# A Mamba scan on one core: three accumulating transfers and a gate moved in the issue order

## The chip, the cores and the metric

The kernel runs on one core of one Trainium2 chip. The metric is the device time of one execution in microseconds (us), lower is better. A profiled execution gives, for each instruction, its engine, start and duration. The engines are PE (matrix multiply, with its weight loads as a row of their own, PEld), DVE (vector), ACT (scalar, activation functions), POOL (general) and SP (issues transfers). Each engine takes its instructions strictly in its own order; an instruction that must wait for a semaphore holds up everything behind it on that engine.

## The reference, cut to what matters

The network has four layers: a double Mamba block, a convolution with attention over taps, a linear attention with a mixture of experts, and a softmax attention with a mixture of experts. The change lies in the first layer alone. What a Mamba block computes, with 512 inner channels, 16 states and sequences of 1024 tokens in 2 images:

```python
delta = softplus(dt @ dt_w + dt_b)
dA = exp(delta[..., None] * A)                      # per token, channel, state
dBu = delta[..., None] * Bm[:, :, None, :] * xs[..., None]
h = dA_t * h + dBu_t                                # a scan over the tokens
y_t = einsum('bdn,bn->bd', h, C_t)                  # sum over the 16 states
y = (y + xs * Dp) * silu(res)                       # res is the gate
out = y @ out_w + out_b
```

The block is applied twice (m1, m2), each time followed by a layer norm and a residual sum.

## The kernel before, in words

**Tiles and units.** The 2048 tokens are cut into 4 chunks of 512, so the two blocks give eight units, numbered 0 to 7 here (m1 chunks 0 to 3, then m2 chunks 0 to 3). `layer0` walks over the units and calls `Mamba.scan` for each.

**One state of a unit.** `scan` loops over the 16 states n. SP loads row n of B, copied to all partitions (tile `b`, L511). POOL multiplies it with `du` (delta times x) into two tiles `h` of two 128-channel blocks each (L515, one product is 128x1024; the tag `h` has six buffers, so three states). For each of the four blocks ACT makes `da` = exp(delta * A) (L524, in PSUM, three buffers), and DVE scans along the tokens, in place in `h` (L528). Then PE turns the four blocks token-side up into PSUM tiles `ht` (L486, three buffers), and each of the four token groups is scaled by C and summed.

**Where the sums go.** The function `rest` chooses. For 10 or 11 of the 16 states DVE adds to `ya` (L501). The states 0, 2, 4, 7 and 10 go through ACT instead (L499): state 0 starts `ya`, state 2 (`ASIDE`) starts a second sum `yb`, and the states 4, 7 and 10 (`ADDED`) write to a tile `m_s` of their own. Accumulating transfers of 1 MB, issued by POOL (L509), add these tiles: `m_s` onto `yb`, `LATER` = 3 states after its own state, and at last `yb` onto `ya`, in the next unit. `self.due` holds for each state number which transfer is due. The tile `yb` has one buffer (pool `m_one`): state 2 of a unit overwrites what the last unit's `yb` onto `ya` transfer reads. `ya` has two buffers.

**Work of other units beside it.** `rest` of state n is drawn on while state n+1 is scanned (`before`), and `between` is a list of generators that `paced` spreads over 63 slots, one slot for each pair of a state and a block. For the unit before there is `back`: its first `NDC` = 4 steps make the gate (PE L556, ACT L560), later ones multiply the sums back with PE (L585, L590), with the gate on DVE (L594) and on to the output. For the unit after there are `enter` and `front`; the last steps of `front` make delta and du: ACT L433 to L450, then POOL L451, L453, L455, L457, in two halves of the channels. The steps left at the end of the loop are drawn after slot 63. The gate's tile shares its one buffer (tag `gate`) with the tile `e` that `front` uses up to L455.

**What sets the order.** The Python order is the wish; a scheduler then orders each engine's instructions by its own estimate of when they are ready. `tc.issue_after(x)` makes it place what stands inside behind x. Waits between engines are semaphores that the framework adds.

Of the kernel before, what the change touches and what calls it, by code (L numbers as in the profile page):

```python
# [14 lines left out]
ALU = mybir.AluOpType  # L15
# [16 lines left out]
NDC = DI // P  # L32
# [219 lines left out]
class Mamba:  # L252
# [208 lines left out]
    def scan(self, j, before, between, start=False, last=False):  # L461

        net, nc, m, scanp = self.net, self.net.nc, self.m, self.scanp
        xs, bd, ct, delta, du = self.chunks[j]
        state, first = self.state, self.first(j)
        ya = self.two.tile([P, TPC, DI], F32, tag="ya", name=f"{m}_ya_{j}")  # L470
        yb = self.one.tile([P, TPC, DI], F32, tag="yb", name=f"{m}_yb_{j}")
        self.chunks[j] = xs, ya, yb
        G = 2
        half = [P, G, TC]

        def keep(n, hs):
            for g, h in enumerate(hs):
                nc.scalar.copy(state[:, n, g * G : (g + 1) * G], h[:, :, TC - 1])

        def rest(n, hs):  # L480


            for i in range(TPC):
                ps = self.ps_ht.tile([P, DI], F32, tag="ht", name=f"{m}_ht_{j}_{n}_{i}")
                for dc in range(NDC):
                    nc.tensor.transpose(  # L486
                        ps[:, dc * P : (dc + 1) * P], hs[dc // G][:, dc % G, i * P : (i + 1) * P],
                        net.ident,
                    )
                yield  # L490
                c = ct[:, i, n : n + 1]
                to = {0: ya, self.ASIDE: yb}.get(n)
                if n in self.ADDED:
                    if i == 0:
                        aside = self.tail(f"{m}_s_{j}_{n}")[:, : TPC * DI]
                        self.due[n + self.LATER] = yb, aside.rearrange("p (i d) -> p i d", d=DI)
                    to = self.due[n + self.LATER][1]
                if to is not None:
                    nc.scalar.activation(to[:, i, :], ps, AF.Copy, scale=c)  # L499
                else:  # L500
                    nc.vector.scalar_tensor_tensor(  # L501
                        ya[:, i, :], ps, c, ya[:, i, :], ALU.mult, ALU.add
                    )
                if i == 0 and first:
                    keep(n, hs)

        for n in range(NS):
            if n in self.due:
                nc.gpsimd.dma_start(*self.due.pop(n), accum_op=ALU.add)  # L509
            b = scanp.tile([P, TC], F32, tag="b", name=f"{m}_b_{j}_{n}", bufs=4)  # L510
            nc.sync.dma_start(b, bd[n].partition_broadcast(P))  # L511
            hs = []
            for g in range(NDC // G):
                h = scanp.tile(half, F32, tag="h", name=f"{m}_h_{j}_{n}_{g}", bufs=6)
                made = (nc.vector if start and n == 0 else nc.gpsimd).tensor_mul(  # L515
                    h, du[:, g * G : (g + 1) * G, :], b.unsqueeze(1).to_broadcast(half)
                )
                hs.append(h)
            self.product = made
            for dc in range(NDC):  # L520
                da = self.ps_da.tile([P, TC], F32, tag="da", name=f"{m}_da_{j}_{n}_{dc}")
                i = dc * NS + n
                with net.tc.issue_after(net.loaded.ins):
                    net.decayed = nc.scalar.activation(  # L524
                        da, delta[:, dc, :], AF.Exp, scale=self.aneg[:, i : i + 1]
                    )
                h = hs[dc // G][:, dc % G, :]
                nc.vector.tensor_tensor_scan(  # L528
                    h, da, h, 0.0 if first else state[:, n, dc : dc + 1], ALU.mult, ALU.add
                )  # L530


                next(before, None)
                if n or dc:
                    next(between, None)
            before = chain(before, rest(n, hs))
        for _ in between:
            pass
        self.due = {} if last else {self.LATER - 1: (ya, yb)}
        return before  # L540

    def tail(self, name):
# [95 lines left out]
def paced(n, parts):  # L638

    taken = [0] * len(parts)  # L640
    for slot in range(n):
        for i, (steps, many, first, end) in enumerate(parts):
            while taken[i] < many and slot >= first + (end - first) * taken[i] / many:
                next(steps, None)
                taken[i] += 1
        yield
    for steps, *_ in parts:
        for _ in steps:
            pass
# [11 lines left out]
def layer0(net, x, x_dram, m1, m2, load_image, taps, conv_dram, lg):  # L661
# [4 lines left out]
    tc, nc = net.tc, net.nc  # L666
    with (
# [28 lines left out]
        def behind(m, steps):  # L696

            while True:
                with tc.issue_after(m.product.ins):
                    if next(steps, steps) is steps:  # L700
                        return
                yield
# [5 lines left out]
        before, done = iter(()), []  # L708
        aside = taps.make(ps_mm, conv_dram)
        for u, (m, j) in enumerate(units):  # L710
            joined = u + 1 < len(units)
            steps = [(b, NDC, 0, 19) for b in done]
            if u:
                m.due.update(units[u - 1][0].due)
            fronts = []
            for a, k in units[u + 1 : u + 2]:
                if k == 0:
                    a.load()
                fronts.append(a.front(k))
                if u == 0:  # L720
                    steps.append((a.enter(k), Mamba.ENTER, 0, 10))
            enters = []
            for a, k in units[u + 2 : u + 3]:
                if k == 0:
                    a.load_in()
                enters.append(a.enter(k))
            steps += [(f, Mamba.HEAD - 3, 0 if u else 10, 25) for f in fronts]
            steps += [(b, NDC + (not joined), 25 if joined else 19, 35) for b in done]
            steps += [(f, 3, 25, 33) for f in fronts]
            if u == NCH - 2:  # L730

                steps.append((behind(m, blocks[1].diagonals()), NDC * 4, 24, 40))
            rest = m.load_rest() if u and j == 0 else iter(())
            steps += [(rest, 1, 37, 38)]
            steps += [(f, Mamba.STEPS, 35, 63) for f in fronts]
            steps += [(b, 4, 36, 50) for b in done]
            steps += [(e, Mamba.ENTER, 44, 62) for e in enters]
            steps += [(b, 3, 54, 62) for b in done]
            steps += [(rest, 1, 62, 63)]
            if u + 1 < len(units):  # L740
                n = 9 if u else 12
                steps += [(islice(aside, n), n, 40, 63)]
            else:
                last.close()
                m.ps_da = last.enter_context(tc.tile_pool(name="m_da2", bufs=2, space=PSUM))
                ps_acc = last.enter_context(tc.tile_pool(name="m_acc", bufs=1, space=PSUM))

                def place(u):
                    pool, tag, w = {
                        3: (one, "pre", TC + 3), 0: (two, "xs", TC), 1: (two, "delta", TC),  # L750
                        2: (two, "du", TC),
                    }[u]
                    a = pool.tile(
                        [P, NDC, w], F32, tag=tag, name=f"early_{u}",
                        bufs=3 if tag == "xs" else None,
                    )
                    return taps.load(u, a.rearrange("p d t -> p (d t)"))

                pair = {u: place(u) for u in taps.ORDER}
                def early():  # L760
                    for k in range(2):
                        a = ps_acc.tile([P, TC], F32, tag="acc", name=f"early_acc{k}")
                        acc = {k: taps.bank(a)}
                        yield from taps.convolve(0, pair, acc)
                        taps.read(acc, lg)

                steps += [(early(), 112, 3, 63)]
            own = m.back(j, u + 1 == len(units), u + 2 < len(units))
            if u + 1 == len(units):

                steps += [(islice(own, 5), 5, 44, 58)]
            before = m.scan(j, before, paced(63, steps), u == 0, u + 1 == len(units))
            done = [own]
# [1091 lines left out]
```

## Time and profile before

| what | us |
|---|---|
| median of 3 runs | 2209.42 |
| lowest and highest run | 2208.55, 2211.64 |
| profiled execution, its time | 2208.24 |
| profiled execution, its span | 2206.5 |
| scans of the eight units, about | 60 to 1106 |
| DVE busy in 60 to 1106 | 874.12 |
| PE busy in 60 to 1106 | 855.52 |
| POOL busy in 60 to 1106 | 781.64 |
| ACT busy in 60 to 1106 | 685.34 |

The page of a profile lists the engines' busy times, the span in 40 slices, the transfer queues, the chain of work that ended last, and the costliest groups of instructions. A timeline lists instructions by start time; the number in brackets is how long the engine sat idle before and which instruction released it. An entry such as `m_ya<-m_yb` is output and input by the program's names with chunk and state numbers left out; where states are named in the text, they are counted along the engine's order.

### The profile page before, as it was taken

What the parts mean: (1) busy time and instruction counts of PE and PEld (TensorE: products, weight loads), DVE (VectorE), ACT (ScalarE), POOL (GpSimd) and SP (SyncE); (2) the same over time, 40 slices, a digit from 0 to 9 for tenths busy, and PEclk for the clock granted to TensorE, in tenths of its full rate; (3) what the DMA queues carried; (4) which work ended last, traced back from release to release, by engine and by line L of the source; (5) the groups of instructions that cost most, each with busy time, mean ns of one, the idle gap of its engine ahead of it and who ended that gap; (6) DMA issues with size and microseconds to landing.
All of it is one profiled execution on the core that took longest, in us unless ns stands there. A gap on an engine that the chain in (4) does not pass through costs nothing.

```text
span 2206.5 us, 26712 instructions
## 1 busy us (share of the span) xinstructions
PE 1876.6 (85%) x9428; PEld 1302.1 (59%) x9428; DVE 1358.1 (62%) x2086; ACT 927.3 (42%) x1658; POOL 1044.1 (47%) x701
## 2 busy tenths in 40 slices
PE   7788787787878878789999999958999699859996
PEld 3455445455444544455566555648999467649994
DVE  6999969698796978978514385652222444442223
ACT  4777577576766757664312253320111122201111
POOL 3897689676886768785314340003332000023331
PEclk9899799797978979799999999969999899969997
DMA  3243323332332322422130100018999200059997
GB/s 106 68 106 82 80 78 83 79 79 64 91 87 67 80 69 69 103 68 64 39 53 0 48 15 0 20 39 311 330 328 348 88 10 10 20 198 321 336 324 283
DMA packets 94959, 256.33 MB, mean 116 GB/s; under 512 B 35963, under 2 KB 52224, under 8 KB 80228
## 3 DMA queue, kind: packets, MB, share of 16 engines
q1 hardware_dynamic: 77636, 198.29, 26.9%
q0 software_dynamic: 12192, 51.66, 10.3%
q10 hardware_dynamic: 4992, 4.59, 0.7%
q8 instruction: 79, 1.29, 0.2%
q14 instruction: 60, 0.49, 0.1%
HBM read 204.60 MB, written 19.37 MB: 102 GB/s over the span
## 4 chain that ended last, share of the span: by engine, by line
PE 33%; issue 7%; DVE 4%; DMA 4%; POOL 4%; ACT 1%; POOLq 0%; ACTq 0%; DVEq 0%
PE h L1672 6%; PE acc L882 4%; PE o L1686 3%; PE av L1396 3%; PE h L1219 3%; PE sc L1370 2%; DMA l_yd<-y,target 2%; POOL x L1642 2%; POOL l_yd L1692 2%; PE w L1228 1%; PE early_acc L882 1%; DMA x<-l_zd,source 1%; PE mm_t L197 1%; PE kvp L1128 1%; PE q L1342 1%
## 5 line engine op out<-in xcount | busy, mean ns | idle before, releaser
L515 POOL TENSOR_TENSOR m_h<-m_du,m_b 128x1024 f32<-128x1024 f32 x254 | 597.9, 2432 | 179.4 <-PE m_ht L486 77.0
L486 PE MATMUL m_ht<-ident,m_h 128*128 128x128 f32 x2048 | 367.3, 306 | 174.0 <-DVE m_ya L501 98.4
L486 PEld LDWEIGHTS m_ht<-ident,m_h 128*128 128x128 f32 x2048 | 260.3, 154 | 364.2 <-DVE m_h L528 126.0
L524 ACT ACTIVATE m_da<-m_delta,m_aneg 128x512 f32<-128x512 f32 x512 | 349.9, 690 | 228.1 <-DVE m_h L528 210.6
L1642 POOL DMA_INDIRECT x<-l_zd,source x82 | 84.2, 1027 | 576.1 <-issue 222.4
L528 DVE TENSOR_TENSOR_SCAN m_h<-m_da,m_state,m_h 128x512 f32<-128x512 f32 x256 | 315.2, 1265 | 54.2 <-POOL m_h L515 47.8
L528 DVE TENSOR_TENSOR_SCAN m_h<-m_da,m_h 128x512 f32<-128x512 f32 x256 | 300.4, 1205 | 53.9 <-POOL m_h L515 42.0
L1672 PEld LDWEIGHTS h<-xts,we 128*128 128x128 f32 x2528 | 297.4, 194 | 7.0 <-issue 3.2
L1672 PE MATMUL h<-xts,we 128*128 128x128 f32 x2528 | 298.4, 277 | 2.4 <-issue 1.9
L501 DVE SCALAR_TENSOR_TENSOR m_ya<-m_ht,m_ct,m_ya 128x512 f32<-128x512 f32 x352 | 253.2, 730 | 53.3 <-PE m_ht L486 52.6
L1678 ACT ACTIVATE hid<-h 128x512 f32<-128x512 f32 x79 | 47.2, 597 | 414.7 <-issue 324.4
L1679 DVE TENSOR_TENSOR hid<-hid,h 128x512 f32<-128x512 f32 x79 | 54.4, 688 | 266.4 <-PE h L1672 266.4
L1686 PE MATMUL o<-we,hid 128*128 128x256 f32 x632 | 150.6, 380 | 3.9 <-DVE hid L1679 2.3
L1692 POOL DMA_INDIRECT l_yd<-y,target x79 | 79.3, 1003 | 136.6 <-DVE y L1691 132.9
L1686 PEld LDWEIGHTS o<-we,hid 128*128 128x128 f32 x632 | 113.7, 190 | 17.8 <-DVE hid L1679 3.0
L367 PE MATMUL m_conv<-m_pre,m_taps 128*128 128x512 f32 x240 | 122.8, 628 | 0.0
L882 PE MATMUL early_acc<-x,early 128*98 128x448 f32 (+24 forms) x308 | 99.9, 451 | 0.4 <-DVE lg L899 0.4
L882 PE MATMUL acc<-x,pair 128*98 128x416 f32 (+21 forms) x308 | 93.0, 450 | 0.0
L556 PE MATMUL m_g<-x,m_gate_sb 128*128 128x512 f32 x128 | 70.3, 674 | 17.7 <-ACT m_gate L560 11.8
L1691 DVE COPY y<-o 128x256 f32<-128x256 f32 x79 | 33.6, 425 | 69.9 <-PE o L1686 69.7
L332 PE MATMUL m_in<-x,m_in_sb 128*128 128x512 f32 x128 | 73.4, 707 | 2.6 <-DVE x L247 1.3
L882 PEld LDWEIGHTS acc<-x,pair 128*98 128x98 f32 x308 | 47.7, 166 | 40.0 <-issue 34.8
(319 smaller groups left out, 2784.4 us busy)
## 6 DMA issues: line engine op xcount, KB each, us to landing
we<-in_l_experts_dram SPq DMA_DIRECT2D x82, 1536.0 KB
m_b<-m_bd SPq DMA_DIRECT2D x128, 256.0 KB
m_yb<-m_s POOLq DMA_DIRECT2D x24, 1024.0 KB
m_ya<-m_yb POOLq DMA_DIRECT2D x7, 1024.0 KB
w<-in_l_w_dram SPq DMA_DIRECT2D x21, 256.0 KB
l_zd<-l_z SPq DMA_DIRECT2D x7, 512.0 KB
l_yl<-l_yd SPq DMA_DIRECT2D x10, 256.0 KB
l_yl<-l_yd ACTq DMA_DIRECT2D x10, 256.0 KB
```

What stands on the lines that cost most here:

```text
L332: nc.tensor.matmul(ps, lhsT=self.in_sb[:, kc, mc * P : (mc + 1) * P], rhs=self.xt[:, kc, tok], start=(kc == 0), stop=(kc == NCC - 1),)
L367: nc.tensor.matmul(ps, lhsT=self.taps[:, dc * 4 + k, :], rhs=pre[:, dc, k : k + TC], start=(k == 0), stop=(k == 3),)
L486: nc.tensor.transpose(ps[:, dc * P : (dc + 1) * P], hs[dc // G][:, dc % G, i * P : (i + 1) * P], net.ident,)
L501: nc.vector.scalar_tensor_tensor(ya[:, i, :], ps, c, ya[:, i, :], ALU.mult, ALU.add)
L515: made = (nc.vector if start and n == 0 else nc.gpsimd).tensor_mul(h, du[:, g * G : (g + 1) * G, :], b.unsqueeze(1).to_broadcast(half))
L524: net.decayed = nc.scalar.activation(da, delta[:, dc, :], AF.Exp, scale=self.aneg[:, i : i + 1])
L528: nc.vector.tensor_tensor_scan(h, da, h, 0.0 if first else state[:, n, dc : dc + 1], ALU.mult, ALU.add)
L882: nc.tensor.matmul(a[:, lo - 16 * k : hi - 16 * k, co : co + n], lhsT=lhsT, rhs=self.x[:, kc, b, lo - r0 : hi - r0, ci : ci + n], start=(u ...
L1642: nc.gpsimd.indirect_dma_start(out=x, out_offset=None, in_=zd[:, :], in_offset=bass.IndirectOffsetOnAxis(ap=source[:, g : g + 1], axis=0), ...
L1672: nc.tensor.matmul(ps[:, at], lhsT=w12[:, s, kc, at], rhs=xt[:, kc * P : (kc + 1) * P], start=(kc == 0), stop=(kc == NCC - 1),)
L1686: nc.tensor.matmul(ps[:, :C], lhsT=ht[:, mc * P : (mc + 1) * P], rhs=w[:, 8 + mc, :], start=(mc == 0), stop=(mc == NHC - 1),)
L1692: nc.gpsimd.indirect_dma_start(out=yd[g], out_offset=bass.IndirectOffsetOnAxis(ap=target[:, g : g + 1], axis=0), in_=y, in_offset=None, bo ...
```

## The change

Three edits. The transfer that is due at a state is now issued after that state's two products, and bound behind the second of them with `issue_after`, where it was issued ahead of the products and free to be placed by the scheduler. The transfer of `yb` onto `ya` is due at state 3 of the next unit, where it was due at state 2. The first four steps of `back`, which make the gate, are spread over the slots 4 to 20, where they had 0 to 19.

```diff
         for n in range(NS):
-            if n in self.due:
-                nc.gpsimd.dma_start(*self.due.pop(n), accum_op=ALU.add)
             b = scanp.tile([P, TC], F32, tag="b", name=f"{m}_b_{j}_{n}", bufs=4)
...
             self.product = made
+            if n in self.due:
+                with net.tc.issue_after(made.ins):
+                    nc.gpsimd.dma_start(*self.due.pop(n), accum_op=ALU.add)
...
-        self.due = {} if last else {self.LATER - 1: (ya, yb)}
+        self.due = {} if last else {self.LATER: (ya, yb)}
...
-            steps = [(b, NDC, 0, 19) for b in done]
+            steps = [(b, NDC, 4, 20) for b in done]
```

## The prediction

> **What bounds the kernel now.** I read the page, then the waits, then the timelines of POOL, ACT and DVE around a change of units. The page's busy times and costliest groups:
>
> ```profile
> PE 1876.6 (85%) x9428; PEld 1302.1 (59%) x9428; DVE 1358.1 (62%) x2086; ACT 927.3 (42%) x1658; POOL 1044.1 (47%) x701
> ...
> L515 POOL TENSOR_TENSOR m_h<-m_du,m_b 128x1024 f32<-128x1024 f32 x254 | 597.9, 2432 | 179.4 <-PE m_ht L486 77.0
> ...
> L528 DVE TENSOR_TENSOR_SCAN m_h<-m_da,m_state,m_h 128x512 f32<-128x512 f32 x256 | 315.2, 1265 | 54.2 <-POOL m_h L515 47.8
> ```
>
> The scans fill 60 to 1106 us; DVE is busy 874.12 of these 1046 us, more than any other engine, and a unit takes some 132 us for about 108 us of DVE work. Inside a unit DVE hardly idles: unit 2 has 1.4, 0.8 and 1.9 us in its first 40 us. The large hole is at the change of units. POOL, then DVE, from unit 1 to unit 2, and POOL from unit 3 to unit 4:
>
> ```profile
> 262.69 2.36 POOL L515 TENSOR_TENSOR m_h<-m_du,m_b 128x1024 f32<-128x1024 f32 x1 [2.82 <-issue]
> 282.28 0.87 POOL L509 DMA_DIRECT2D m_ya<-m_yb  x1 [17.23 <-DVE m_ya L501]
> 282.87 2.67 POOL L451 TENSOR_TENSOR m_du<-m_e,m_du 128x1024 f32<-128x1024 f32 x1
> ...
> 297.43 3.52 DVE L528 TENSOR_TENSOR_SCAN m_h<-m_da,m_h 128x512 f32<-128x512 f32 x3 [15.45 <-POOL m_h L515]
> ...
> 548.29 2.36 POOL L451 TENSOR_TENSOR m_du<-m_e,m_du 128x1024 f32<-128x1024 f32 x1 [17.31 <-ACT m_du L450]
> ```
>
> The accumulating transfer stands on POOL ahead of L451 and waits for the last sum; the chain L451 to L457 and the product for blocks 2 and 3 follow, and DVE waits 15.45 us. This is the wait that the change takes away (66.6 us over four changes of units, among POOL's waits). The last line is the control: from unit 3 to 4 the scheduler had already put the transfer behind L457, and POOL sits idle as long, for ACT's L450.
>
> The other end of the transfer is ACT's write of state 2 into `yb`, which has one buffer. POOL and ACT in unit 1, where the transfer stands directly behind the products of state 2:
>
> ```profile
> 170.32 0.83 POOL L509 DMA_DIRECT2D m_ya<-m_yb  x1
> ...
> 177.00 0.69 ACT L524 ACTIVATE m_da<-m_delta,m_aneg 128x512 f32<-128x512 f32 x1 [0.54 <-DVE m_h L528]
> 177.63 0.67 ACT L560 ACTIVATE m_gate<-m_g,cols_sb 128x512 f32<-128x512 f32 x1
> 178.77 1.27 ACT L499 ACTIVATE m_yb<-m_ht,m_ct 128x512 f32<-128x512 f32 x2 [0.48 <-DMA m_ya<-m_yb]
> ```
>
> ACT waits for the transfer, 0.48 us, already with an issue at state 2: 8.45 us from issue to release.
>
> **Edit 1: the transfer to its new place, what it removes.** In the changed program's order POOL has, at the change of units, L451, L629, L453, L455, L629, L457. The transfer's wait goes; next late is ACT's L450, which feeds L451:
>
> ```profile
> 280.94 1.17 ACT L450 ACTIVATE m_du<-m_du,minus_one 128x1024 f32<-128x1024 f32 x1
> ```
>
> It ends at 282.11, the last sum (L501) at 281.98. L451 can start about 0.08 us behind L450 (548.22 to 548.30 in unit 4), so at 282.19, not 282.87: 0.68 us won. By the same rows it is 0.88 in unit 3, 0.75 in unit 5, 0.69 in unit 6. POOL's chain to the end of L457 takes 12.1 to 12.25 us beside the transfer and 11.84 without (unit 4): another 0.3. In unit 4 one issue of 0.6 and the slower product behind it go, 0.8 us. Units 1 and 7 have the transfer in POOL's slack: nothing. Gain: 1.0 + 1.2 + 0.8 + 1.05 + 1.0 = 5.0 us. It cannot be more unless L450 came earlier, and ACT's order at the end of a unit is unchanged.
>
> **Edit 1: what it adds.** The transfer now stands behind the second product of state 3. Let T be the start of the unit's first scan of block 2. POOL makes products without a pause from there in units 2 to 6, 2.32 us each, so state 3 ends at T+13.9 (297.43 to 311.29 in unit 2, 13.8 to 13.9 in 3 to 6); for units 1 and 7, taking the 0.6 to 0.8 us of the old issue off, 13.2 and 14.0. From issue to the last of its 144 packets the seven transfers took 8.06, 8.34, 7.26, 6.98, 7.25, 8.35 and 8.21 us in the trace: mean 7.8, and 0.1 to the release. So ACT's first write to `yb` can start at T+21.8. Its place in ACT's new order is behind `da` of state 3, block 2, which in unit 2 was made at T+15.4 to 16.1:
>
> ```profile
> 312.06 0.69 ACT L499 ACTIVATE m_yb<-m_ht,m_ct 128x512 f32<-128x512 f32 x1 [0.86 <-PE m_ht L486]
> 312.65 0.28 ACT L478 COPY m_state<-m_h 128x2 f32<-128x2 f32 x2
> 312.82 0.69 ACT L524 ACTIVATE m_da<-m_delta,m_aneg 128x512 f32<-128x512 f32 x1
> 313.45 0.67 ACT L499 ACTIVATE m_yb<-m_ht,m_ct 128x512 f32<-128x512 f32 x1
> 314.02 0.69 ACT L524 ACTIVATE m_da<-m_delta,m_aneg 128x512 f32<-128x512 f32 x1
> ```
>
> ACT would stand there from about T+16 to T+22. Queued behind on ACT is the `da` of block 3, for which DVE waits; on PE the `ht` tiles fill (three buffers) and its order stops at the fourth of state 2. DVE has only the scans whose `da` is made. Next scan: T + 13.9 + 7.9 + two writes (1.15) + one `da` (0.69) + 0.05 = T+23.7, against the old start of that scan:
>
> - units 2, 3, 4, 5: old T+18.8, 18.9, 17.7, 18.7, so 4.9, 4.8, 6.0, 5.0 us lost;
> - unit 6, where the new order has the first write ahead of block 2's `da` and a gate piece behind the second: T+25.1 against 18.3, 6.8 us;
> - unit 1: 13.2 + 7.9 + 1.15 + 0.74 = 23.0 against 19.9, 3.1 us;
> - unit 7, one write ahead of the `da`: 14.0 + 7.9 + 0.57 + 0.74 = 23.2 against 19.3, 3.9 us.
>
> Sum 34.5 us. With the shortest and longest packet times seen, 7.0 and 8.35, it is 29 and 38. Behind the stop DVE again runs from scan to scan (ACT makes a `da` in 0.6 us, a scan takes 1.12 to 1.2), so the loss stays; POOL's state 5 and 6 products, which wait for PE to leave `h`, come 3 to 5 us before their scans. In unit 7 PE is busy 19 to 20 us of every 20 from 985 on, and stops only some 2 of the 3.9 us: I take 1.0 off there (0 to 2).
>
> The skill's page "DMA: Bandwidth & Descriptors", section "Anatomy of one DMA — SWDGE (gpsimd) path", fits one transfer as 2.0 us and the bytes at 436 GB/s. For 1 MB that is an estimate of 4.4 us, where the rows have 7.0 to 8.35 (these transfers also read what they add to). By it the loss would be 34.5 less 7 x 3.4, so 10.7, and the sum of all terms +8 us. The rows decide. The same page's "Rules for kernel authors" advises to issue a transfer early and to wait for it late, which speaks against this edit: the issue moves by a state, the wait does not.
>
> **Edit 2: the other 24 transfers.** 20 keep their place between the same products. In units 3 and 5 the one of state 4 goes ahead of the first product of state 8, 2.3 us earlier, into an idle of 1.45 us; in unit 2 and the like it passes two small multiplications of 0.6 us. POOL has 1.5 to 3 us of idle per state there. Taken at 0, with one issue (0.85 us) per unit as the bound either way.
>
> **Edit 3: the gate from slot 4.** The same 28 activations of 0.69 us and 56 matmuls come about a state later. At the change of units ACT no longer stands 6.45 us for L455 before its first piece, but DVE waits for POOL's product there, which lies behind L455 anyway: 0. The silu of the gate now comes ahead of all four writes of state 4, so two of them (1.25 us) move in between the two table loads at state 6, where DVE already idled 1.87 us for `da`. In their old place these two held up the `da` ahead of the loads by some 0.6 us, so the stretch grows by about 0.6 us net in each of units 2 to 6: 3.0 in all (0 to 6).
>
> **Sum.** +34.5 + 3.0 - 1.0 - 5.0 = +31.5 us on the profiled execution's 2208.24, which stands 1.2 below the median 2209.42. I forecast 2240 for the median. From the bounds: 29 + 0 - 2 - 5 = +22 to 38 + 6 - 5 = +39, with 4 either way for edit 2.
>
> **Rivals.**
> - *The wait removed is all that counts* (faster): if POOL were far enough ahead, the transfer would land before ACT needs `yb`. It decides from where state 3's products end at T+16 - 7.9 = T+8.1 or sooner, 5.8 us before the row. Speaks for it: POOL idles 1.5 to 3 us per state later in a unit. Against: right behind the change of units it has no pause to give up. Then only the gain of 5.0 us is left: 2204. 8%.
> - *The stop is partly made up*: the stop falls into the same unit as 3 to 5 us of other DVE idle (PE's `ht` at states 14 and 15), and ACT is busy in only 685 of the 1046 us. If half is made up, +14: 2223. Against: ACT's and PE's places at a unit's end follow DVE's scans. 15%.
> - *The stop costs more*: PE's stop delays convolutions and the gate, so that the silu stretch slides too, 2 us more per unit: 2254. 5%.
> - *Nothing moves*, gain and loss equal: 2209. 4%.
>
> **How the numbers follow.** The main case has 68%; with the partial and the dearer case, slower has 88%. Within 0.2% (4.4 us, about what a measurement of this kernel can tell from no change) 4%, faster 8%. The range 2221 to 2255 holds the main case's bounds, the half made up and the dearer one.
>
> **What the changed profile would show.** Right: a wait of ACT `m_yb` for the transfer `m_ya<-m_yb` of 4 to 7 us in each of seven units, some 35 us in all; DVE's waits for `da` up by as much; POOL's 66.6 us wait for L501 gone and one for ACT L450 of nearly the same size in its place; DVE's idle at the change of units still 13 to 15 us. Wrong: L451 starting well before the last sum, or ACT's wait under 2 us; then POOL ran ahead or the transfer landed faster than any row here shows.

## The result and the profile after

The changed kernel takes 2244.68 us (median of 4 runs, 2243.6 to 2246.13), the kernel before 2209.02 beside it (4 runs). The ratio is 1.0159, with a 95% interval of 1.0142 to 1.0177. The profiled execution has a span of 2242.6 us where before had 2206.5, so it is 36.1 us longer.

The page of the changed kernel, its busy times and the two groups shown of before (columns: executions and shape, busy and mean ns of one, idle time ahead and what ended most of it):

```profile
PE 1880.2 (84%) x9428; PEld 1306.9 (58%) x9428; DVE 1357.8 (61%) x2086; ACT 924.6 (41%) x1658; POOL 1042.8 (47%) x701
...
L513 POOL TENSOR_TENSOR m_h<-m_du,m_b 128x1024 f32<-128x1024 f32 x254 | 598.1, 2412 | 219.5 <-PE m_ht L486 95.7
...
L529 DVE TENSOR_TENSOR_SCAN m_h<-m_da,m_state,m_h 128x512 f32<-128x512 f32 x256 | 316.7, 1267 | 70.9 <-POOL m_h L513 45.3
```

The engines do the same work in the same time (DVE 1357.8 against 1358.1). So the 36 us are waiting, not work: ahead of the products POOL idles 219.5 where it had 179.4. (L513 and L529 are the old L515 and L528; the transfer is L520.)

The changed kernel's waits (engine and line that waited, what it waited for, us in all, how often, the longest):

```profile
POOL m_h L513 <- PE m_ht L486: 95.7, 26, 14.2
...
DVE m_h L529 <- POOL m_h L513: 84.8, 11, 14.4
POOL m_du L451 <- ACT m_du L450: 83.8, 7, 17.2
...
DVE m_h L529 <- ACT m_da L525: 55.5, 24, 6.5
...
ACT m_yb L499 <- DMA m_ya<-m_yb: 45.6, 7, 8.5
```

The old wait of POOL for the last sum, 66.6 us, is gone from the list. In its place POOL waits 83.8 us for ACT's L450, where that was 18.4 (one change of units and two trifles). ACT's wait for the transfer, which was one of 0.5 us, comes seven times, once in each of the units 1 to 7, and DVE's waits for `da` went from 18.2 to 55.5.

One unit in full, the timelines of ACT, POOL and DVE from the change between units 1 and 2 to the stop (start, duration, engine; in brackets the idle time ahead and its releaser):

```profile
285.39 1.16 ACT L450 ACTIVATE m_du<-m_du,minus_one 128x1024 f32<-128x1024 f32 x1
...
286.63 2.35 POOL L451 TENSOR_TENSOR m_du<-m_e,m_du 128x1024 f32<-128x1024 f32 x1 [17.05 <-ACT m_du L450]
...
300.89 5.84 DVE L529 TENSOR_TENSOR_SCAN m_h<-m_da,m_h 128x512 f32<-128x512 f32 x5 [14.45 <-POOL m_h L513]
...
314.66 0.83 POOL L520 DMA_DIRECT2D m_ya<-m_yb  x1
...
318.47 2.32 DVE L529 TENSOR_TENSOR_SCAN m_h<-m_da,m_h 128x512 f32<-128x512 f32 x2
...
323.24 1.26 ACT L499 ACTIVATE m_yb<-m_ht,m_ct 128x512 f32<-128x512 f32 x2 [6.11 <-DMA m_ya<-m_yb]
...
325.12 2.34 DVE L529 TENSOR_TENSOR_SCAN m_h<-m_da,m_h 128x512 f32<-128x512 f32 x2 [4.32 <-ACT m_da L525]
```

L451 starts with ACT's L450, the change of units is 1.0 us shorter (14.45 for 15.45), and then the transfer, issued 13.8 us behind the first scan of block 2 (T = 300.89), holds ACT until T+22.35 and DVE for 4.32 us. The other units have the same picture: DVE's new idle ahead of the scan of state 3, block 3 (in unit 6 of block 2) is 3.55, 4.32, 5.08, 5.19, 4.63, 6.46 and 3.62 us in units 1 to 7, 32.9 in all.

**How the difference is measured below.** Single profiles differ outside the change too: up to the first T (unit 1) by up to 2.2 us, and in the stages behind the Mamba block, where nothing was changed, by -1.6 to +5.7 us against before. So beside each median stands the *window*: the time from the T of unit 1 to the last gate multiplication of unit 7, in the profiled execution. Before has 951.8 us there, the changed kernel 986.3, so +34.5 of the 36.1.

| kernel | median us | ratio (95%) | window against before | DVE idle at the six changes of units |
|---|---|---|---|---|
| before | 2209.02 | | 951.8 | 79.7 |
| after | 2244.68 | 1.0159 (1.0142, 1.0177) | +34.5 | 74.5 |
| e1 due at state 1 | 2246.94 | 1.0157 (1.0123, 1.0191) | +35.3 | 81.5 |
| e2 `yb` started by state 3 | 2221.17 | 1.0048 (1.0030, 1.0065) | +11.0 | 74.4 |
| e3 before, bound | 2213.91 | 1.0010 (1.0000, 1.0019) | +1.3 | 74.6 |
| e4 before, gate from slot 4 | 2213.49 | 1.0015 (1.0006, 1.0025) | +0.9 | 79.6 |
| e5 state 1, behind the last sum | 2212.87 | 1.0012 (1.0000, 1.0024) | +3.9 | 74.5 |
| e6 e5 with the old gate | 2212.37 | 1.0013 (1.0004, 1.0022) | -0.3 | 74.5 |
| e7 due at state 2 | 2223.20 | 1.0065 (1.0050, 1.0081) | +11.5 | 74.5 |
| e8 after, old gate | 2240.99 | 1.0148 (1.0132, 1.0163) | +31.6 | 74.5 |
| e9 e6 with the norm from slot 50 | 2187.74 | 0.9895 (0.9879, 0.9912) | -16.9 | 42.5 |
| e10 before, norm from slot 50 | 2188.79 | 0.9902 (0.9885, 0.9920) | -12.6 | 44.1 |
| e11 due at state 4 | 2254.74 | 1.0211 (1.0196, 1.0226) | +47.0 | 74.6 |
| e12 e10, transfers at 3, 6, 9 | 2163.97 | 0.9788 (0.9775, 0.9802) | -51.6 | 44.0 |

### The profile page after: what moved, and what is told of

Its sections match the earlier page's. It is cut to its first block, busy times and chain, and to the rows that moved or that the text cites. A ratio compares the mean times of both kernels' runs of the same rounds, so it can differ in the third digit from the quotient of the medians.

```text
span 2242.6 us, 26709 instructions
## 1 busy us (share of the span) xinstructions
PE 1880.2 (84%) x9428; PEld 1306.9 (58%) x9428; DVE 1357.8 (61%) x2086; ACT 924.6 (41%) x1658; POOL 1042.8 (47%) x701
## 3 DMA queue, kind: packets, MB, share of 16 engines
q8 instruction: 79, 1.29, 0.3%
## 4 chain that ended last, share of the span: by engine, by line
PE 32%; issue 6%; DVE 4%; DMA 4%; POOL 4%; ACT 1%; POOLq 0%; ACTq 0%; DVEq 0%
PE h L1673 6%; PE acc L883 3%; PE o L1687 3%; PE av L1397 3%; PE h L1220 2%; PE sc L1371 2%; DMA l_yd<-y,target 2%; POOL x L1643 2%; POOL l_yd L1693 2%; PE w L1229 1%; PE early_acc L883 1%; DMA x<-l_zd,source 1%; PE mm_t L197 1%; PE kvp L1129 1%; PE o L1042 1%
## 5 line engine op out<-in xcount | busy, mean ns | idle before, releaser
L513 POOL TENSOR_TENSOR m_h<-m_du,m_b 128x1024 f32<-128x1024 f32 x254 | 598.1, 2412 | 219.5 <-PE m_ht L486 95.7
L529 DVE TENSOR_TENSOR_SCAN m_h<-m_da,m_state,m_h 128x512 f32<-128x512 f32 x256 | 316.7, 1267 | 70.9 <-POOL m_h L513 45.3
L529 DVE TENSOR_TENSOR_SCAN m_h<-m_da,m_h 128x512 f32<-128x512 f32 x256 | 301.0, 1205 | 69.7 <-POOL m_h L513 39.6
L367 PE MATMUL m_conv<-m_pre,m_taps 128*128 128x512 f32 x240 | 123.0, 639 | 1.4 <-ACT m_tail L627 1.1
L332 PE MATMUL m_in<-x,m_in_sb 128*128 128x512 f32 x128 | 74.5, 715 | 2.6 <-DVE x L247 1.3
L451 POOL TENSOR_TENSOR m_du<-m_e,m_du 128x1024 f32<-128x1024 f32 x14 | 33.2, 2372 | 83.8 <-ACT m_du L450 83.8
```

Of the source, the lines that this page charges most:

```text
L332: nc.tensor.matmul(ps, lhsT=self.in_sb[:, kc, mc * P : (mc + 1) * P], rhs=self.xt[:, kc, tok], start=(kc == 0), stop=(kc == NCC - 1),)
L367: nc.tensor.matmul(ps, lhsT=self.taps[:, dc * 4 + k, :], rhs=pre[:, dc, k : k + TC], start=(k == 0), stop=(k == 3),)
L529: nc.vector.tensor_tensor_scan(h, da, h, 0.0 if first else state[:, n, dc : dc + 1], ALU.mult, ALU.add)
```

## The experiments

The theory on trial: the loss is ACT's wait for the transfer ahead of its first write to `yb`, and it follows the time of issue. The main rival: it comes from the binding, from the traffic or from the gate.

**e1: the transfer two states earlier.** In the changed kernel:

```diff
-        self.due = {} if last else {self.LATER: (ya, yb)}
+        self.due = {} if last else {1: (ya, yb)}
```

> The changed kernel, but the transfer of yb onto ya is due at state 1 instead of state 3 (still bound behind that state's products). Theory (ACT's write to yb waits for a transfer issued too late): issue at about T+4.6 in units 2 to 6, release at about T+13.2, ahead of ACT's need at T+15.5, so the waits of m_yb for m_ya<-m_yb fall from 45.6 us to under 2 us and the time to 2207 us (2203 to 2213). Rival (the binding of the transfers or the later gate is what costs): the time stays near 2240 us although the wait is gone.

It missed: 2246.94, as slow as the changed kernel and near the rival's 2240. But neither theory named what happened: ACT no longer waits, and DVE does instead. The timeline of POOL and DVE in unit 2 of e1, and below it the line of e1's waits:

```profile
307.88 0.85 POOL L520 DMA_DIRECT2D m_ya<-m_yb  x1
...
311.08 2.48 DVE L529 TENSOR_TENSOR_SCAN m_h<-m_da,m_h 128x512 f32<-128x512 f32 x2 [1.88 <-ACT m_da L525]
317.25 0.75 DVE L501 SCALAR_TENSOR_TENSOR m_ya<-m_ht,m_ct,m_ya 128x512 f32<-128x512 f32 x1 [3.69 <-DMA m_ya<-m_yb]
```

```profile
DVE m_ya L501 <- DMA m_ya<-m_yb: 28.2, 7, 6.2
```

The sum at 317.25 is the last one of the unit before: state 15, token group 3. `rest` of state 15 is drawn with the first scans of the new unit, and its fourth sum is emitted with the second state's first block. At state 1 the program issues the transfer before that sum, so the sum must wait until the transfer has landed in the same `ya`. The run moved the wait from ACT to DVE and did not test what it was meant to.

**e5 and e6: state 1 again, behind the last sum.** The transfer due at state 1 is issued after block 0 of that state; e6 also puts the gate back to the slots 0 to 19:

```diff
-            if n in self.due:
+            if n in self.due and n != 1:
...
                 if n or dc:
                     next(between, None)
+                if n == 1 and dc == 0 and n in self.due:
+                    with net.tc.issue_after(made.ins):
+                        nc.gpsimd.dma_start(*self.due.pop(n), accum_op=ALU.add)
...
-        self.due = {} if last else {self.LATER: (ya, yb)}
+        self.due = {} if last else {1: (ya, yb)}
...
-            steps = [(b, NDC, 4, 20) for b in done]
+            steps = [(b, NDC, 0, 19) for b in done]
```

> The changed kernel with the transfer of yb onto ya due at state 1 and issued behind state 1's first block, so that the last sum of the unit before is already ahead of it in the program and need not wait for it. POOL issues at about T+4.6 (T is the unit's first scan of block 2), the transfer ends at about T+13.2, ahead of ACT's first write to yb at T+14 to T+17. My theory (the loss is ACT's wait for the transfer): the wait is gone, the 5.0 us at the changes of units stay won, the gate from slot 4 costs the 4.3 us that it cost alone: 2209 (2204 to 2214), with no wait of m_yb for the transfer over 1 us in units 2 to 6. Rival (the loss comes from the transfer standing bound behind a product, or from its traffic beside the other transfers): 2230 to 2245.

> As the run before, with the gate at the slots 0 to 19 as in the kernel before. My theory: only the gain at the changes of units is left, 2209.2 less 5.0: 2204 (2200 to 2209), faster than the kernel before. Rival (the gain of 5.0 us is eaten by the chain of L450 and later waits): 2209 to 2213.

e5 has 2212.87, in my range, and ACT waits for the transfer once, 0.8 us. Undoing nothing but the time of issue gives back 30.6 of the window's 34.5 us. e6 has 2212.37, outside my range and inside the rival's: the 5.2 us at the changes of units are there (74.5 for 79.7), but the window is only 0.3 us shorter, and that in the fastest of its eleven runs; the median is 3 us above before's beside it. Where they went shows in the timelines of e6, DVE and ACT in unit 2 (L564 is the gate's activation, L560 its matmuls):

```profile
304.92 1.22 DVE L529 TENSOR_TENSOR_SCAN m_h<-m_da,m_h 128x512 f32<-128x512 f32 x1 [1.00 <-ACT m_da L525]
...
305.53 0.69 ACT L564 ACTIVATE m_gate<-m_g,cols_sb 128x512 f32<-128x512 f32 x1 [0.71 <-PE m_g L560]
...
307.40 1.22 DVE L529 TENSOR_TENSOR_SCAN m_h<-m_da,m_h 128x512 f32<-128x512 f32 x1 [1.26 <-ACT m_da L525]
```

In before PE ran the matmuls of the second gate piece (293.3 to 297.0) and eight of the convolution's (L367) inside the hole at the change of units. In e6's order that piece runs behind T (303.0 to 305.5) and only four of the convolution's in the hole; ACT waits for PE three times in this stretch (0.50, 0.44 and 0.71 us), and DVE behind ACT. This is read from one unit.

**e7 and e11: state 2 and state 4.** In the changed kernel, e7:

```diff
-        self.due = {} if last else {self.LATER: (ya, yb)}
+        self.due = {} if last else {self.LATER - 1: (ya, yb)}
```

and e11 the same with `LATER + 1`.

> The changed kernel with the transfer of yb onto ya due at state 2: issued at about T+9.2 behind the products of state 2, released after 8.65 us at T+17.9; ACT's first write stands behind da of state 3, block 2 (until about T+16), so ACT waits about 2 us in place of 6.5, and the scan of state 3, block 3 starts 4.65 us earlier than in the changed kernel, in no unit before its old start. My theory: 2244.7 less 3.6 (unit 1), 4.65 x 5 and 3.7 (unit 7), about 2214 (2209 to 2219). Rival (the loss does not follow the time of issue): 2230 to 2245.

> The changed kernel with the transfer of yb onto ya due at state 4: issued a state later again, about T+18.5, released at T+27.2. ACT's first write to yb stands behind da of state 5, block 0 or 1 in this program, so DVE has up to six scans more (7 us) before ACT's order stops it, but PE's three ht tiles and POOL's six h tiles fill before that, since the sums of state 2 wait. My theory: as much again as from state 2 to state 3 (21.5 us), 2266 (2255 to 2280). Rival (the later place of the write in ACT's order makes up for the later issue): 2238 to 2250.

e7: issue at T+9.2, ACT's wait 14.7 us in seven units for 45.6, window +11.5 for +34.5. The median, 2223.2, is 4 above my range and outside the rival's: the loss follows the time of issue. In the profile's unit 2 the scan of state 3, block 3 starts at T+19.65 as forecast. The units 4 to 6 are 2.6, 4.1 and 3.4 us longer than before; no single wait carries it (1.94 us of the stop in unit 6, a few tenths to 1.3 us each at states 6, 9 and 10). e11: 2254.74, a hair below my range and above the rival's. The waits of e11:

```profile
PEld m_ht L486 <- ACT m_yb L499: 45.2, 9, 6.8
...
PE m_ht L486 <- ACT m_yb L499: 38.7, 7, 6.3
...
POOL m_h L513 <- ACT m_yb L499: 28.1, 3, 9.4
...
ACT m_yb L499 <- DMA m_ya<-m_yb: 16.6, 7, 3.4
```

The write stands later in ACT's order, so ACT waits less itself (16.6), but PE's `ht` tiles fill behind it and PE waits for it. More than half of the later issue is made up (+12.4 in the window, where 4.6 us in each of seven units are 32). So, with the gate from slot 4, the windows go +3.9 (e5, issue at T+4.5 in units 2 to 6), +11.5 (e7, T+9.2), +34.5 (T+13.8) and +47.0 (e11, T+18.4); with the old gate they go -0.3 (e6), +1.3 (e3, below) and +31.6 (e8). The steepest step in both is from state 2 to state 3. In units 2 to 5 ACT comes to the write at T+15.0 to T+16.2 with the gate from slot 4 and at T+17.0 to T+18.2 with the old one; a transfer due at state 2 lets it start at T+17.7 to T+18.0, one due at state 3 at T+22.3 to T+22.9.

**e2: the same transfer, a later first write.** In the changed kernel the second sum is started by state 3:

```diff
-    ASIDE = 2
+    ASIDE = 3
```

> The changed kernel with the transfer where the change puts it, but yb is first written by state 3 instead of state 2 (ASIDE 3; state 2 is summed on DVE instead). Theory: the release at about T+22.4 is as before, the need moves from T+16 to about T+21, behind the da of state 4; ACT's wait falls from 6.5 to 1 to 3 us per unit, with made da in hand: 2215 us (2207 to 2225). Rival (the place of the issue on POOL or the gate costs, not who waits for the transfer): 2235 to 2245 us.

2221.17, in the range. The transfer is issued and lands as in the changed kernel, and ACT has no wait for it. So neither the place on POOL nor the traffic costs what the changed kernel lost. What remains (+11.0) is not the stop; 1.0 to 1.3 us more idle ahead of the second scan of state 6 in each of units 2 to 5 are part of it (2.9 for 1.6 to 1.9), and in unit 7 DVE idles 5.9 us ahead of the second scan of state 5, for 1.7; the rest was not traced.

**e3, e4, e8: the parts alone.** e3 is the kernel before with the transfers bound behind the products, still due at state 2; e4 is before with the gate from slot 4; e8 is the changed kernel with the old gate. e3 against before, then e4 against before, then e8 against the changed kernel:

```diff
-            if n in self.due:
-                nc.gpsimd.dma_start(*self.due.pop(n), accum_op=ALU.add)
...
+            if n in self.due:
+                with net.tc.issue_after(made.ins):
+                    nc.gpsimd.dma_start(*self.due.pop(n), accum_op=ALU.add)
```

```diff
-            steps = [(b, NDC, 0, 19) for b in done]
+            steps = [(b, NDC, 4, 20) for b in done]
```

```diff
-            steps = [(b, NDC, 4, 20) for b in done]
+            steps = [(b, NDC, 0, 19) for b in done]
```

> The kernel before with the transfers bound behind the products of their state and nothing else: yb onto ya still due at state 2, the gate from slot 0. Theory: issue at T+9.2 in units 2 to 6, release at T+17.8; the write to yb stands behind all four da of state 3, so nearly nothing waits; the wait for the last sum goes but L451 then waits for L450, so 5 us are won and 0 to 7 lost: 2208 us (2203 to 2214). Rival (the wait taken off POOL is worth its 66.6 us, or the 15 us of DVE's at each change of units): 2150 to 2190 us.

> The kernel before with only the gate's four steps in slots 4 to 20. Theory: the silu stretch at state 6 grows by about 0.6 us in five units and nothing else moves: 2212 us (2208 to 2217). Rival (the later gate is a main part of the 35.7 us): 2220 us or more.

> The changed kernel with the gate at the slots 0 to 19 as before, the transfer still due at state 3. ACT's first write to yb then stands behind da of state 3, block 3 in units 2 to 5 (in the changed kernel behind block 2), so one scan more (1.2 us) runs before DVE stops; in unit 6 and 7 one to two. My theory: 2244.7 less 4.3 (what the gate cost alone) less 1.2 x 4, 2.4 and 1.2: 2232 (2226 to 2240). Rival (the gate's cost and the stop do not meet, only the 4.3 go): 2240.

e3 has 2213.91 and e4 2213.49, inside my ranges and outside the rivals'. Both medians are 4 to 5 us above before's, but the window says +1.3 and +0.9, and 3.6 and 5.7 us of their profiles, which in both are of the slowest of ten runs, lie in the stages behind. Binding alone also wins the 5.1 us at the changes of units and gives them back inside the units, as e6 does. e8 has 2240.99: with the transfer due at state 3 the gate's new place costs 2.9 us in the window, and 4.2 between e6 and e5, near the 3.0 forecast.

Between e3 and e7, which differ in the gate alone, the same move costs some 10 us. ACT's waits for the transfer in e3, e7 and e8:

```profile
ACT m_yb L499 <- DMA m_ya<-m_yb: 2.3, 3, 1.3
...
ACT m_yb L499 <- DMA m_ya<-m_yb: 14.7, 7, 4.0
...
ACT m_yb L499 <- DMA m_ya<-m_yb: 34.4, 7, 6.0
```

With the old gate ACT's first write stands behind all four `da` of state 3 in units 2 to 5, with the gate from slot 4 behind three. Due at state 2, the transfer ends in this gap, so the gate's place decides whether ACT waits; due at state 3, ACT waits in both orders. e8 missed my 2232, which had put one scan more ahead of the stop, some 8 us, on the credit side: the stop in units 1 to 6 is 24.7 us for 29.2, and in unit 2 it has only moved to the next scan (4.70 us ahead of state 4, for 4.32 ahead of the last scan of state 3).

**e9 and e10: what ends the change of units.** The norm's steps from slot 50, in e6 and in the kernel before:

```diff
-            steps += [(b, 3, 54, 62) for b in done]
+            steps += [(b, 3, 50, 62) for b in done]
```

> The kernel of run e6 (transfer at state 1 behind the last sum, gate at the slots 0 to 19) with the norm's three steps spread from slot 50 where they had 54. ACT's scaling of the norm (L186) then stands one state earlier in its order and L450 of the second half two da earlier, ahead of the next unit's first da. My theory (behind the transfer's wait, ACT's L450 is what POOL waits for at the change of units): L451 starts some 3 us earlier at each of five changes, DVE's idle there falls from 13.4 to 14.5 us to about 11, 15 us in all, of which the waits behind it take back up to the half, as in e6: 2201 (2196 to 2209). Rival (the change of units is set by the last sum and what PE does, L450 only happens to end there): 2210 to 2216.

> The kernel before with the norm from slot 50 alone. My theory: POOL's transfer still stands ahead of L451 and waits for the last sum, so an earlier L450 changes nothing in units 2, 3, 5 and 6; only unit 4, where the transfer stands behind L457, can win some 3 us: 2207 (2203 to 2213). Rival (the transfer's wait binds nothing, L450 alone does): 2199 to 2203, as run e9.

Both are 20 to 21 us faster than before, more than either theory expected. The timelines of POOL and DVE, e10, change from unit 1 to 2:

```profile
281.96 2.37 POOL L451 TENSOR_TENSOR m_du<-m_e,m_du 128x1024 f32<-128x1024 f32 x1 [1.29 <-ACT m_du L450]
...
284.66 2.34 DVE L528 TENSOR_TENSOR_SCAN m_h<-m_da,m_h 128x512 f32<-128x512 f32 x2
...
295.15 3.52 DVE L528 TENSOR_TENSOR_SCAN m_h<-m_da,m_h 128x512 f32<-128x512 f32 x3 [8.16 <-POOL m_h L515]
```

L451 still starts with ACT's L450, but now 2.6 us ahead of the last sum's end (284.5), and DVE's idle is 8.16 for 15.45. Over the six changes 79.7 us become 42.5 and 44.1. e10 does not do what I wrote for it: in its built program the scheduler puts the transfer behind L457 or behind products of its own accord, so POOL has no wait for the sum left, and the run does not tell whether that wait alone would have bound. The window moves by less than half of what the changes of units win (12.6 of 35.6 us in e10). A hazard of the same kind shows in e10's waits and in its ACT timeline:

```profile
ACT m_tail L186 <- DMA m_yb<-m_s: 37.8, 7, 7.3
```

```profile
655.22 1.93 ACT L186 ACTIVATE m_tail<-m_out,ln_off,ln_rs 128x256 f32<-128x256 f32 x4 [7.29 <-DMA m_yb<-m_s]
```

L186 writes into the one-buffer tile `tail` that the transfer of state 10 still reads. In before this wait was 2.2 us in all.

**e12: that transfer a state earlier.** In e10:

```diff
-    ADDED = 4, 7, 10
+    ADDED = 3, 6, 9
```

> Run e10 (the kernel before, norm from slot 50) with the states that are summed by transfer at 3, 6 and 9 where they were 4, 7 and 10. In run e10 ACT's L186 waits 37.8 us in seven units for the last of these transfers, which leaves the tile that L186 writes; a state earlier (some 7 us) the transfer has landed. My theory: DVE's waits of 4.3 us at state 14 and of 1.8 to 2.2 us beside it shrink, 5 to 10 us in all: 2180 (2174 to 2188). Rival (states 2 and 3 both on ACT, with the gate, cost as much at the start of a unit as the end wins): 2186 to 2200.

2163.97 us, 2.1% faster than before and the best of all, 10 us below the low end of my range. L186 waits for no transfer any more (37.8 us in e10). What is left is the change of units, DVE's largest wait among the scans of e12:

```profile
DVE m_h L528 <- POOL m_h L515: 52.1, 9, 10.2
```

The changes of units stay at 44.0. The window is 39.0 us shorter than e10's: in units 1 to 6 DVE idles 78 us for 107, and is busy 7 us less (not explained); unit 7 is 2.6 us shorter. In unit 4 the 4.3 us ahead of state 14 and 2.75 us ahead of a sum in mid unit are gone, and so are the 1.5 to 2.3 us ahead of the second scan of state 6 in units 1, 3 and 5. This last part I had not forecast: the writes that shared ACT with the silu at state 6 now come a state earlier. e12 is one edit on e10, so the sum of the parts is shown; how it splits was only read from one profile of each.

## Why the prediction held

The forecast was 2240 (2221 to 2255), slower with 0.88. It came to 2244.68. Step by step, in the window:

- **Gain at the changes of units, 5.0.** Right, to its parts: 1.00, 1.29, 0.78, 1.19 and 0.96 us in units 2 to 6, together 5.2. Its reason held too: ACT's L450 ends within 0.15 us of the last sum in units 2, 3, 5 and 6. e9 and e10 move L450, and the holes close by 37.2 and 35.6 us against before. What the step overlooked is that the hole was covering other work: e6 has the gain and keeps 0.3 us of it. DVE's small waits between T and the second scan of state 2 are 3.9 us in units 2 to 6 of before, and 7.7 in e3, 8.1 in e6 and 7.0 in e8, which have the old gate.
- **The stop, 34.5.** Right in mechanism and place, mis-sized by one term. The scan of state 3, block 3 starts 3.64, 5.44, 5.33, 7.07, 5.66, 7.30 and 4.39 us later against T than before, 38.8 in all. The term *7.8 us of packets and 0.1 to the release* was too small: these transfers took 8.28 us on average from issue to last packet (8.15 to 8.72), and ACT started about 0.4 us behind that. That is 0.78 us in each of seven units, 5.5, against the 4.3 missing. The 0.4 could have been read before: the row of unit 1 has 8.45 us from issue to ACT's start, and the packets of that transfer took 8.06.
- **The gate, 3.0.** Near: 3.0 us more idle around state 6 in units 1 to 6 (from the scan of state 5, block 2 to that of state 7, block 2: 19.2 for 16.2), and 2.9 us by e8. What the step did not count is unit 7, where DVE idles 1.3 us more around state 5, with the gate alone (e4) as well. *At the change of units: 0* held: in e4 the small waits behind T stay at 3.9 us. In the changed kernel they are 7.6, but ahead of the stop, which ends when the transfer does, they add nothing.
- **Edit 2, 0.** Not tested by itself; e3, which binds these transfers together with the first, has +1.3 in all.
- **Less 1.0 in unit 7.** Wrong: unit 7's end comes 5.4 us later, more than the 4.39 of its scan, with the gate's 1.3 us behind it.

The window's 34.5 us are 29.1 in units 1 to 6 and these 5.4. In units 1 to 6 DVE's idle time grew by 29.6 us: 29.7 at the stop, 3.8 in the small waits ahead of it, 3.0 around state 6, less 5.2 at the changes of units and 1.7 in the rest of the units. The sign to look for, a wait of ACT of some 35 us in all, came as 45.6; ACT comes to the write earlier than DVE runs out of scans, so the scans lose less than ACT waits (32.9).

Of the rivals, *the wait removed is all that counts* needed the issue at T+8.1 or sooner. e7 at T+9.2 still has ACT waiting 14.7 us and e5 at T+4.5 has 0.8, so its point was well placed; but its price was wrong, since even e6 is no faster than before. *The stop is partly made up* is excluded by the window, and *the stop costs more* by the stretch around state 6, which grew by 3.0 us in six units and not by 2 in each. The estimate of 4.4 us for such a transfer, from the fit on the Trainium skill's page "DMA: Bandwidth & Descriptors" (section "Anatomy of one DMA — SWDGE (gpsimd) path"), does not fit this case: the shortest of the seven took 8.15 us in the changed kernel. The same page's advice to issue early and wait late ("Rules for kernel authors") agrees with e5, e7, the changed kernel and e11 in this order; e1, issued as early as e5 but ahead of a sum that needs its target, gains nothing by it.

## What to carry to other kernels

A wait that is taken off one engine is worth the distance to the next thing that is late, here 1.0 to 1.3 us where 17 us of waiting stood in the profile; look for what else ends at that moment before counting the wait as gain, and for what work was done inside the hole. A transfer that reads a one-buffer tile is a lease on the next write to it: sum the place of issue and the whole time from issue to landing, and compare it with the writer's place, including what stands behind the writer on its in-order engine. Other work in that engine's order moves the writer's place: the gate's move cost 0.9 us alone and some 10 where it also brought the write ahead of the transfer's end. The gain was at the other end of both: moving the step that feeds the late instruction (the norm, 4 slots) and the last transfer off its tile (one state) brought 2.1%, where moving the waiting transfer brought nothing.

## What was not expected of the hardware

An accumulating transfer of 1 MB between two tiles took 8.15 to 8.72 us from issue to last packet at this place. The other 24 in the same profile took 6.5 to 9.1, eight of them under 7.0; no run here tells what makes these shorter. The instruction that waited for the transfer began about 0.4 us after its last packet. And profiles of kernels that differ only in the first 1150 us differ by up to 7.3 us in the later stages (1091.3 to 1098.6 us), so that a difference of 4 us in one profiled execution, as in e3 and e4, can lie wholly outside the change.
